# Merged products for shared edge tiles, split last units and a node-major output in a four-layer sparse graph network

## The chip, the cores and the metric

The kernel runs on one core of one Trainium2 chip. The metric is the device time of one execution in microseconds, and the figure for a kernel is the median of its runs. A profile is one further execution, taken with the hardware profiler.

## The reference

The input is `x`, 8 batches of 2048 nodes with 128 features each, and `adj`, one 2048 x 2048 matrix of 0 and 1. It is symmetric, has ones on its diagonal and about 16 ones in a row. Four layers follow one another; layers 0 and 2 are of one kind, 1 and 3 of another.

An attention layer (0 and 2) computes, in each batch,

```
Q, K, V = h Wq, h Wk, h Wv                       (8 heads of 16)
attn    = softmax over the neighbours m of n of Q[n].K[m] / 4
x       = LN1(h + (attn V) Wo + bo)
out     = LN2(x + relu(x W1 + b1) W2 + b2)
```

A graph layer (1 and 3) computes

```
h   = x W
e   = leaky_relu(h[i].a_src + h[j].a_dst)        for neighbours j of i
out = LN(x + softmax(e) h)
```

LN is a layer norm over the 128 features. All arithmetic is float32. The result is the output of layer 3, of shape (8, 2048, 128).

## The kernel before, in words

**Units and edge tiles.** The kernel doesn't use the dense adjacency. It first makes lists of neighbours from `adj`, and then works on 32 units of 64 nodes (`UNIT`, `NU`). On chip a unit's features are 128 rows: two halves of 64 rows, one for batches 0 to 3 and one for batches 4 to 7 (`HB` is 4, and `hf` counts the halves). Its columns are 4 batches x 128 features. A unit's nodes are two groups of 32 (`GROUP`, counted by `j`). Each group has edge tiles of 128 edges, and a unit has nine (`TILES`): four steps with one tile for each group, and a fifth step whose one tile is shared by both groups (`tiles = 1 if t == TG - 1 else 2`). An edge tile is gathered from a table in device memory, one row for one edge, by an indirect DMA that GpSimd issues (`gather`, L1469). The row of a node holds all 8 batches: keys and values for an attention layer (8 KB), or features with their two scores for a graph layer (4160 bytes).

**Attention layer.** For each step `spread` (L1542) multiplies one-hot matrices with the queries, so that each edge has its node's query in PSUM. VectorE multiplies it with the gathered keys (L1554) and sums over the head's 16 features (L1561). ScalarE takes the exponential (L1571). GpSimd or VectorE weighs the values with it (L1580). `add` (L1615) sums the edges of each node: a one-hot matrix of 128 edges x 32 nodes is multiplied with the weighted values and with the weights. For each group `j` and half `hf` this goes to its own strip of 32 rows of `acc` and `sums`.

**Graph layer.** VectorE and ScalarE make the weight of each edge and batch (L1788 to L1800), `fold` (L1810) multiplies the one-hot columns with them into `w`, and `add` (L1825) multiplies `w` with the gathered rows: for each batch, group and half one product of 128 edges x 32 nodes with 129 columns. For odd units the accumulators lie in the PSUM buffer `q` (four banks, one buffer), for even units in `acc` and `sums` (one bank each). Gathered rows of a graph layer go into a ring: one `kv` buffer holds four tiles, and there are six.

**After the sums.** `after_attention` (from L1626) divides, transposes, multiplies by Wo, adds the residual (`add_to`, L1649), normalises, runs the two-matrix network and normalises again. `after_graph` (from L1837) divides, adds the centred input (L1865) and normalises. In a norm, `centred` multiplies with a centring matrix on TensorE, `squares` takes each batch's variance (L1406 to L1409), `root` the inverse root (L1416, L1417), and four operations scale the four batches (L1439, L1441). Then `keep` (L1228) stores the unit's features in device memory (`xd`), `project` (L1328) multiplies with the next layer's weights, copies the rows out of PSUM into one of two `trows` buffers, and stores them in the next layer's table (L1392). In layer 3 the result, 64 nodes x 4 batches x 128 features for each half, is stored to the output instead (L1886), one 512-byte piece for each node and batch.

Most products of this part go to the PSUM tag `m`, which has two buffers of one bank. Operations after the sums run on ScalarE, except in the last two units of a layer (`late`), where `either` lets ScalarE or VectorE take them.

**What sets the order.** Operations are not issued where they are written. `op` records each with its estimated cost on each engine that can do it, a key (layer, then unit, then step), and the buffers it reads, writes or takes. `Plan.order` (L643) then runs a list scheduling: it keeps a clock, gives every free engine the ready operation of the lowest key for which the buffers are free, and so fixes each engine's order for the whole program. For the tags in `BY_KEY` buffers are given out in order of the keys. On the chip each engine follows this order. A gather of a layer reads the whole table of that layer, so that it waits until the last unit of the layer before has stored its rows.

Of the kernel before, what the change touches and what calls it, by code (L numbers as in the profile page):

```python
# [9 lines left out]
F32 = mybir.dt.float32  # L10
# [6 lines left out]
ALU = mybir.AluOpType  # L17
# [3 lines left out]
P = 128  # L21
H = 8
# [19 lines left out]
WIDE = DEG + 5  # L42
STRIDE = 1000
# [22 lines left out]
class Dense:  # L66
# [460 lines left out]
    def batch(self, b):  # L527
        x = self.two.tile([P, self.NB, P], F32, name="x")
        self.nc.sync.dma_start(out=x, in_=self.x_in[b].rearrange("(t p) d -> p t d", p=P))
        for n, kind in enumerate(LAYERS):  # L530
            if kind is MHA:
                units = 2 * self.NB * (self.N // QC)
                gen = self.attention(x, n)
            else:
                units = self.NB * self.NC
                gen = self.graph(x, n)
            for u in gen:
                yield u / units
        self.nc.sync.dma_start(out=self.out[b].rearrange("(t p) d -> p t d", p=P), in_=x)
# [14 lines left out]
class Cell:  # L554


    def __init__(self, tag=None, make=None):
        self.tag, self.make = tag, make
        self.tile = None
        self.writers, self.readers = [], []  # L560
        self.left = 0
        self.owner = None

# [11 lines left out]
class Plan:  # L575
# [12 lines left out]
    def __init__(self, nc):  # L588
        self.engines = {
            "PE": nc.tensor,  # L590
            "DVE": nc.vector,
            "ACT": nc.scalar,
            "POOL": nc.gpsimd,
            "SP": nc.sync,
        }
        self.ops = []
        self.bufs = {}
        self.pools = {}
        self.lines = set()
# [11 lines left out]
    def op(self, costs, fn, key, reads=(), writes=(), joins=(), holds=(), shares=(), port=False, dma=0):  # L611


        o = Op(costs, fn, key, port, dma)
# [127 lines left out]
class Sparse:  # L742
# [15 lines left out]
    def __init__(self, ctx, tc, x, xt, adj, w, out):  # L758
# [22 lines left out]
        self.late = False  # L781
        self.gates = {}
# [407 lines left out]
    def slots(self, e, hot, owner):  # L1190
# [3 lines left out]
            hot.tile[:, GS:HOT].rearrange("p (j t c) -> p t j c", j=2, t=TG),  # L1194
# [30 lines left out]
    def keep(self, u, x, key):  # L1225
        self.op(
            {"SP": 0.45},
            lambda e: e.dma_start(out=self.xd[u], in_=x.tile),  # L1228
            key,
            reads=[x],  # L1230
            writes=[self.x_at[u]],
            dma=P * CH * 4,
        )
# [51 lines left out]

    def copy(self, e, out, in_):
        if e is self.nc.scalar:
            e.copy(out, in_)  # L1288
        else:
            e.tensor_copy(out, in_)  # L1290

    def transposed(self, x, key, out, tag="m"):

        ps = self.cell(tag, [P, CH], name="ps_t")

        def run(e):
            for b in range(self.HB):
# [5 lines left out]
    def centred(self, x, key, *out):  # L1303

        ps = self.cell("m", [P, CH], name="ps_c")

        def run(e):
            for b in range(self.HB):
# [6 lines left out]
    def product(self, w, x, key, name, out):  # L1315

        ps = self.cell("m", [P, CH], name=name)
# [10 lines left out]
    def project(self, n, u, x, key, of=None, shares=()):  # L1328
# [5 lines left out]
        rows = self.cell(("trows", "hidden", "trows")[u % 3] if n == 0 else "trows", [P, hb * width], name="trows")  # L1334
        for v in range(2):
            tag = ("m", "m", "acc", "m", "m", "sums")[(2 * u + v) % 6] if n == 0 else "m"
            ps = self.cell(tag, [P, 2, 256], name="ps_p")

            def products(e, ps=ps, v=v):
                for b in range(2):  # L1340
                    cols = slice((2 * v + b) * P, (2 * v + b + 1) * P)
# [11 lines left out]
            if mha:  # L1353
# [9 lines left out]
                    writes=[rows],  # L1363
                )
            else:

                def fill(e, ps=ps, v=v):
# [10 lines left out]
                    writes=[rows],  # L1378
# [7 lines left out]
                    writes=[self.t_at[u]],  # L1386
                )

# [9 lines left out]
    def norm(self, r, key):  # L1398

        hb = self.HB  # L1400
        var = self.cell("var", [P, hb, 2])
# [9 lines left out]
        for b in range(hb):  # L1411
            self.op(self.either(0.55, 0.4), lambda e, b=b: squares(e, b), key, reads=[r], joins=[var])
        rstd = self.cell("rstd", [P, hb])
# [6 lines left out]
        normed = self.cell("normed", [P, hb, P])  # L1420
        for b in range(hb):
# [21 lines left out]
    def scaled(self, rows, gamma, beta, tag, key):  # L1443
        x = self.cell(tag, [P, CH])
# [46 lines left out]
    def attention(self, n):  # L1491
# [3 lines left out]
        for u in range(self.NU):  # L1495
# [14 lines left out]
            for t in range(TG):  # L1510
# [39 lines left out]
                op({"PE": 1.2}, spread, key - 6, reads=[q, hot], writes=[qe])  # L1550
# [52 lines left out]
                def add(e, t=t, kv=kv, hot=hot, acc=acc, sums=sums, part=part, exps=exps, tiles=tiles):  # L1603
# [6 lines left out]
                    for out, rhs in ((acc.tile, part(kv, 1)), (sums.tile, weights)):  # L1610
                        for j in range(2):
                            for hf in range(2):
                                rows = slice((2 * hf + j) * GROUP, (2 * hf + j + 1) * GROUP)
                                col = GS + (j * TG + t) * GROUP
                                e.matmul(  # L1615
                                    out[rows, :],
                                    lhsT=hot.tile[:, col : col + GROUP],
                                    rhs=rhs[:, 2 * (j % tiles) + hf, :],
# [5 lines left out]
            self.after_attention(n, u, acc, sums, x, base)  # L1624

    def after_attention(self, n, u, acc, sums, x, base):  # L1626
        self.late = u >= self.NU - 2
        L, hb = self.layers[n], self.HB
        op, cell = self.op, self.cell
        key = base + TG  # L1630
        rc = cell("rc", [P, hb * H])

        op({"DVE": 0.35}, lambda e: e.reciprocal(rc.tile, sums.tile), base, reads=[sums], writes=[rc])
        a = cell("rows", [P, hb, P], name="a")

        def divide(e):
            e.tensor_tensor(
                a.tile.rearrange("p b (h d) -> p (b h) d", d=HD),
                acc.tile.rearrange("p (c d) -> p c d", d=HD),
                rc.tile.unsqueeze(2).to_broadcast([P, hb * H, HD]),  # L1640
# [5 lines left out]
        def add_to(r, ps, bias, other, key):  # L1646
            op(
                {"DVE": 0.72},
                lambda e: e.scalar_tensor_tensor(r.tile, ps.tile, bias, other.tile, ALU.add, ALU.add),  # L1649
# [5 lines left out]
        at = cell("at", [P, CH])  # L1655
        ps = self.transposed(a, key, at)
        op(self.either(0.6, 0.68), lambda e, ps=ps: self.copy(e, at.tile, ps.tile), key, reads=[ps], writes=[at])
        r = cell("r", [P, CH], name="r1")
        ps = self.product(L["Wo"], at, key, "ps_o", r)
        add_to(r, ps, L["bo"], x, key - 2)  # L1660
        normed = self.norm(self.centred(r, key), key)
        x1 = self.scaled(normed, L["ln1_g"], L["ln1_b"], "x1", key)
        hidden = cell("hidden", [P, FFN // P, CH])
# [10 lines left out]
        r = cell("r", [P, CH], name="r2")  # L1674
        ps = cell("m", [P, CH], name="ps_y")
# [23 lines left out]
    def graph(self, n):  # L1699
# [3 lines left out]
        for u in range(self.NU):  # L1703
# [49 lines left out]
            if u % 2:  # L1753
# [13 lines left out]
            for i, t in enumerate(steps):  # L1767
# [36 lines left out]
                w = cell("w", [P, 2, 2 * hb, GROUP])  # L1804

                def fold(e, t=t, hot=hot, e8=e8, w=w, tiles=tiles):
                    oh = hot.tile[:, GS:HOT].rearrange("p (j t c) -> p j t c", j=2, t=TG)[:, :, t, :]
                    for j in range(0, 2, tiles):
                        shape = [P, tiles, 2 * hb, GROUP]
                        e.tensor_tensor(  # L1810
                            w.tile[:, j : j + tiles],
# [8 lines left out]
                def add(e, kv=kv, w=w, acc=acc, both_rows=both_rows, tiles=tiles, first=i == 0, last=i == TG - 1):  # L1820
                    for b in range(hb):
                        for j in range(2):
                            for hf in range(2):
                                rows = slice((2 * hf + j) * GROUP, (2 * hf + j + 1) * GROUP)
                                e.matmul(  # L1825
                                    acc(b)[rows, :],
                                    lhsT=w.tile[:, j, hf * hb + b, :],
                                    rhs=both_rows(kv)[:, j % tiles, hf * hb + b, 1 : P + 2],
# [6 lines left out]
            self.after_graph(n, u, outs, banks, acc, x, base)  # L1835

    def after_graph(self, n, u, outs, banks, acc, x, base):  # L1837
        self.late = u >= self.NU - 2
        L, hb = self.layers[n], self.HB
        op, cell = self.op, self.cell  # L1840
        key = base + TG

        rc = cell("rc", [P, hb], name="rcg")

        def inverse(e):
            for k, bank in enumerate(banks):
# [5 lines left out]
        a = cell("rows", [P, hb, P], name="a")  # L1852
        for b in range(hb):
            op(
                self.either(0.37, 0.28),
                lambda e, b=b: self.scale(e, a.tile[:, b, :], acc(b)[:, 0:P], rc.tile[:, b : b + 1]),
# [4 lines left out]
        r = cell("r", [P, CH])  # L1861
        ps = self.centred(x, key, r, a)
# [12 lines left out]
        else:  # L1875

            def last(e):
                shape = [P, 4, P]
# [5 lines left out]
            def store(e):  # L1884
                for part, nodes, hf in self.parts(u):
                    e.dma_start(  # L1886
                        out=self.out[hf * hb : (hf + 1) * hb, nodes, :].rearrange("b p d -> p b d"),
# [3 lines left out]
            op({"SP": 0.9}, store, key, reads=[normed], dma=P * CH * 4)  # L1891
# [101 lines left out]
```

## Time and profile before

| | us |
|---|---|
| median of 3 runs | 3263.28 |
| lowest and highest run | 3248.8, 3274.68 |
| the profiled execution's own time | 3296.99 |
| its span, first to last instruction | 3295.2 |
| layer 0, from the first gather (L1469) to the first of layer 1 | 136.2 to 1225.0 |
| layer 1, to the first gather of layer 2 | 1225.0 to 1789.7 |
| layer 2, to the first gather of layer 3 | 1789.7 to 2726.4 |
| layer 3, to the last output store's issue | 2726.4 to 3280.2 |

The page's mean granted TensorE clock is 0.867 of the full one. The DMA queue filled by the gathers moves 864 MB in 166,464 packets, the other data queue 155 MB in 94,464. TensorE's float32 products appear in the trace as two records each, and each has its own weight load ("PEld").

In the stage view each row is a stretch of time, with the busy microseconds and the number of instructions of each engine in it. In the timeline a row has a start, a duration, the engine, the line of the kernel, the operation, and what it writes and reads; "x8" merges eight records, and the square brackets say how long the engine had been idle before and what ended that. In the view of waits a row says which line waited for which, the total, how often, and the longest.

### The profile page before, as it was taken

What the parts mean: (1) busy time and instruction counts of PE and PEld (TensorE: products, weight loads), DVE (VectorE), ACT (ScalarE), POOL (GpSimd) and SP (SyncE); (2) the same over time, 40 slices, a digit from 0 to 9 for tenths busy, and PEclk for the clock granted to TensorE, in tenths of its full rate; (3) what the DMA queues carried; (4) which work ended last, traced back from release to release, by engine and by line L of the source; (5) the groups of instructions that cost most, each with busy time, mean ns of one, the idle gap of its engine ahead of it and who ended that gap; (6) DMA issues with size and microseconds to landing.
All of it is one profiled execution on the core that took longest, in us unless ns stands there. A gap on an engine that the chain in (4) does not pass through costs nothing. (4 is left out here: it accounts for less than half of the span.)

```text
span 3295.2 us, 63421 instructions
## 1 busy us (share of the span) xinstructions
PE 2532.1 (77%) x23624; PEld 1474.1 (45%) x23624; DVE 2311.1 (70%) x3617; ACT 1399.5 (42%) x4894; POOL 2104.5 (64%) x1447
## 2 busy tenths in 40 slices
PE   6777888878878866788876788888887785777675
PEld 5633444444334334565654233334443343555454
DVE  4789889878878763444444998998989873445554
ACT  4435455555444422444443244444444441333333
POOL 0168777777878835555563777878787835555552
PEclk8769889899999977888898899999999996778877
DMA  7868879887889749999997989999998848899994
GB/s 252 304 228 325 313 285 370 308 337 292 321 321 347 301 156 322 347 327 332 324 352 257 358 331 376 356 353 350 357 354 351 352 186 281 289 317 313 312 302 160
DMA packets 261246, 1023.15 MB, mean 310 GB/s; under 512 B 40193, under 2 KB 69633, under 8 KB 189025
## 3 DMA queue, kind: packets, MB, share of 16 engines
q0 software_dynamic: 166464, 864.44, 70.4%
q1 hardware_dynamic: 94464, 154.56, 13.7%
q8 instruction: 190, 3.11, 0.4%
q14 instruction: 128, 1.04, 0.1%
HBM read 978.59 MB, written 88.08 MB: 324 GB/s over the span
## 5 line engine op out<-in xcount | busy, mean ns | idle before, releaser
L1469 POOL DMA_INDIRECT kv<-table,idx x1152 | 1191.3, 1034 | 931.7 <-issue 395.9
L1580 POOL TENSOR_TENSOR kv<-kv 128x2048 f32<-128x2048 f32 (+1 forms) x252 | 900.0, 3584 | 76.8 <-ACT kv L1571 72.9
L1554 DVE TENSOR_TENSOR kv<-qe,kv 128x2048 f32<-128x2048 f32 (+1 forms) x320 | 662.7, 2071 | 184.6 <-DMA kv<-table,idx 117.2
L1561 DVE TENSOR_REDUCE s<-kv 128x128 f32<-128x2048 f32 (+1 forms) x320 | 659.4, 2061 | 11.4
L1542 PE MATMUL qe<-q_sb,hot 32*128 32x512 f32 (+1 forms) x2304 | 400.2, 700 | 193.7 <-DVE kv L1554 183.5
L1615 PE MATMUL acc<-kv,hot 128*32 128x512 f32 x2560 | 371.4, 658 | 55.1 <-POOL kv L1580 49.6
L1810 DVE TENSOR_TENSOR w<-hot,e 128x512 f32<-128x512 f32 (+1 forms) x384 | 222.2, 597 | 163.6 <-ACT e L1800 83.0
L1825 PE MATMUL acc_q<-kv,w 128*32 128x129 f32 x5120 | 264.7, 314 | 93.7 <-issue 66.7
L1825 PE MATMUL acc<-kv,w 128*32 128x129 f32 x2560 | 155.1, 330 | 135.2 <-issue 89.1
L1825 PEld LDWEIGHTS acc_q<-kv,w 128*32 128x32 f32 x5120 | 177.3, 124 | 166.7 <-issue 117.5
L1542 PEld LDWEIGHTS qe<-q_sb,hot 32*128 32x128 f32 (+1 forms) x2304 | 106.7, 197 | 319.3 <-DVE kv L1554 247.8
L1571 ACT ACTIVATE kv<-s 128x128 f32<-128x128 f32 (+1 forms) x320 | 95.1, 298 | 313.7 <-DVE s L1561 190.8
L1825 PE MATMUL sums<-kv,w 128*32 128x129 f32 x2560 | 171.6, 319 | 58.0 <-issue 57.3
L1406 ACT ACTIVATE junk<-ps_c 128x128 f32<-128x128 f32 x496 | 137.4, 277 | 175.6 <-PE ps_c L1310 116.0
L1288 ACT COPY trows<-ps_p 128x258 f32<-128x258 f32 (+1 forms) x230 | 108.3, 473 | 223.8 <-PE ps_p L1345 90.5
L1615 PEld LDWEIGHTS sums<-kv,hot 128*32 128x32 f32 x2560 | 88.8, 118 | 217.9 <-issue 214.6
L1320 PE MATMUL ps_f<-x,W 128*128 128x512 f32 x256 | 156.8, 700 | 20.5 <-ACT x L1449 12.1
L1825 PEld LDWEIGHTS acc<-kv,w 128*32 128x32 f32 x2560 | 86.4, 127 | 186.4 <-issue 120.0
L1800 ACT ACTIVATE e<-e 128x16 f32<-128x16 f32 (+1 forms) x320 | 65.6, 211 | 219.9 <-DVE e L1795 124.5
L1310 PE MATMUL ps_c<-centre,r 128*128 128x128 f32 x1024 | 145.7, 287 | 14.9 <-DVE r L1649 10.9
L1310 PEld LDWEIGHTS ps_c<-centre,r 128*128 128x128 f32 x1024 | 125.9, 194 | 67.1 <-DVE r L1649 32.3
L1679 PE MATMUL ps_y<-hidden,W 128*128 128x512 f32 x256 | 145.7, 654 | 3.3 <-DVE kv L1580 1.7
(170 smaller groups left out, 4052.4 us busy)
## 6 DMA issues: line engine op xcount, KB each, us to landing
table<-trows SPq DMA_DIRECT2D x128, 256.0 KB
xd<-xnew SPq DMA_DIRECT2D x96, 256.0 KB
x<-xd SPq DMA_DIRECT2D x96, 256.0 KB
kv<-table,idx POOLq DMA_INDIRECT x1152
table<-trows SPq DMA_DIRECT2D x128, 130.0 KB
kv<-adj_dram SPq DMA_DIRECT2D x16, 1024.0 KB
kv<-xt_dram SPq DMA_DIRECT2D x8, 1024.0 KB
x<-xt_dram SPq DMA_DIRECT2D x32, 256.0 KB
```

Source lines behind the costliest of these rows:

```text
L1310: e.matmul(ps.tile[:, cols], lhsT=flat(x.tile)[:, cols], rhs=self.centre, start=True, stop=True)
L1320: lambda e: e.matmul(ps.tile, lhsT=w, rhs=x.tile, start=True, stop=True),
L1406: e.activation(self.junk, x, AF.Square, scale=P**-0.5, accum_out=var.tile[:, b, 1:2])
L1469: e.indirect_dma_start(out=rows(kv.tile, j), out_offset=None, in_=self.tables[n], in_offset=bass.IndirectOffsetOnAxis(ap=self.idx[:, u, co ...
L1542: e.matmul(qe.tile[:, j, hf, :], lhsT=hot.tile[rows, t * P : (t + 1) * P], rhs=q.tile[rows, :], start=True, stop=True,)
L1554: e.tensor_tensor(k, qe.tile[:, 0:tiles].rearrange("p j h c -> p (j h) c"), k, ALU.mult)
L1561: e.tensor_reduce(s.tile[:, 0 : tiles * heads].rearrange("p (q c) -> p q c", q=2 * tiles), k, axis=mybir.AxisListType.X, op=ALU.add,)
L1580: e.tensor_tensor(v, v, w.unsqueeze(3).to_broadcast([P, 2 * tiles, heads // 2, HD]), ALU.mult)
L1615: e.matmul(out[rows, :], lhsT=hot.tile[:, col : col + GROUP], rhs=rhs[:, 2 * (j % tiles) + hf, :], start=(t == 0 and out is acc.tile), sto ...
L1679: lambda e, f=f, ps=ps: e.matmul(ps.tile, lhsT=L["W2"][:, f, :], rhs=hidden.tile[:, f, :], start=(f == 0), stop=(f == FFN // P - 1),),
L1810: e.tensor_tensor(w.tile[:, j : j + tiles], oh[:, j : j + tiles].unsqueeze(2).to_broadcast(shape), e8.tile[:, 0:tiles].unsqueeze(3).to_bro ...
L1825: e.matmul(acc(b)[rows, :], lhsT=w.tile[:, j, hf * hb + b, :], rhs=both_rows(kv)[:, j % tiles, hf * hb + b, 1 : P + 2], start=first and b ...
```

## The change

The change has three parts.

1. **One product for a shared tile.** Both groups' one-hot columns of a step now stand beside one another (in `hot`, and in `w` for the graph layers). Where a step's tile is shared, `add` makes one product with 64 output rows for each half, in place of two with 32 rows.
2. **The last unit's operations in two halves of the batches.** `in_halves` calls `after_attention` or `after_graph` twice for unit 31 of each layer: for batches 0 and 1 of each half, then for batches 2 and 3. Every operation has then half the columns; costs for the scheduling are multiplied by 0.55. Both use the same buffers on chip, each its part of the columns (`rows`, `Part`). The first half's products go to `m` as before, the second half's to `q` (`bank`). Rows go to the table when both halves are there. To leave `q` free for this, even units of a graph layer now accumulate in `q`, and odd ones (31 is odd) in `acc` and `sums`; and the scheduling lets `spread` of an attention layer start only when the layer's table is complete.
3. **Output by node.** The output lies in device memory as (node, batch, feature), so that a store of four batches writes 2048 bytes in one piece for each node (1024 in the halves of the last unit). The host returns a transposed view.

```diff
@@ class Plan / op
-        o = Op(costs, fn, key, port, dma)
+        o = Op({e: us * self.share for e, us in costs.items()}, fn, key, port, dma)
+        shares = [*shares, *(c.whole for c in (*reads, *writes, *joins, *holds) if c.whole)]
@@ slots
-            hot.tile[:, GS:HOT].rearrange("p (j t c) -> p t j c", j=2, t=TG),
+            hot.tile[:, GS:HOT].rearrange("p (t j c) -> p t j c", j=2, t=TG),
@@ new
+    def in_half(self, v, made):
+        self.blocks, self.made, self.at, self.plan.share = range(2 * v, 2 * v + 2), made, 0, 0.55
...
+    def bank(self, name, shape=None):
+        shape = shape or [P, len(self.blocks) * P]
+        if self.made is None or not self.blocks.start:
+            return self.cell("m", shape, name=name)
...
+        return Part(self.cell("q", [P, QB, CH], name=name + "_q"), cut)
@@ project
+        if halves[-1] == 0:
+            return
         def store(e):
@@ attention: spread
-                op({"PE": 1.2}, spread, key - 6, reads=[q, hot], writes=[qe])
+                op({"PE": 1.2}, spread, key - 6, reads=[q, hot, self.table[n]], writes=[qe])
@@ attention: add
-                        for j in range(2):
+                        for j in range(tiles):
                             for hf in range(2):
-                                rows = slice((2 * hf + j) * GROUP, (2 * hf + j + 1) * GROUP)
-                                col = GS + (j * TG + t) * GROUP
+                                at = (2 * hf + j) * GROUP
+                                rows = slice(at, at + GROUP * (3 - tiles))
+                                col = GS + (2 * t + j) * GROUP
                                 e.matmul(
                                     out[rows, :],
-                                    lhsT=hot.tile[:, col : col + GROUP],
-                                    rhs=rhs[:, 2 * (j % tiles) + hf, :],
+                                    lhsT=hot.tile[:, col : col + GROUP * (3 - tiles)],
+                                    rhs=rhs[:, 2 * j + hf, :],
...
-            self.after_attention(n, u, acc, sums, x, base)
+            self.in_halves(u, lambda: self.after_attention(n, u, acc, sums, x, base))
+
+    def in_halves(self, u, after):
+        self.late = u >= self.NU - 2
+        if u < self.NU - 1:
+            after()
+            return
+        made = []
+        for v in range(2):
+            self.in_half(v, made)
+            after()
+        self.whole()
@@ graph
-            if u % 2:
+            if u % 2 == 0:
                 outs = [cell("q", [P, 4, CH], name="acc_q")]
...
-                w = cell("w", [P, 2, 2 * hb, GROUP])
+                w = cell("w", [P, 2 * hb, 2, GROUP])
@@ graph: add
-                        for j in range(2):
+                        for j in range(tiles):
...
-                                    acc(b)[rows, :],
-                                    lhsT=w.tile[:, j, hf * hb + b, :],
-                                    rhs=both_rows(kv)[:, j % tiles, hf * hb + b, 1 : P + 2],
+                                    acc(b)[at : at + GROUP * (3 - tiles), :],
+                                    lhsT=w.tile[:, hf * hb + b, j : j + 3 - tiles, :].rearrange("p j c -> p (j c)"),
+                                    rhs=both_rows(kv)[:, j, hf * hb + b, 1 : P + 2],
@@ after_graph: store
+                    batches = slice(hf * hb + blocks.start, hf * hb + blocks.stop)
                     e.dma_start(
-                        out=self.out[hf * hb : (hf + 1) * hb, nodes, :].rearrange("b p d -> p b d"),
+                        out=self.out[nodes, batches, :],
                         in_=normed.tile[part],
                     )
```

## The prediction

> **What bounds the kernel now.** I read the page first (busy shares and the chain that ended last), then busy time by stage, then the timeline at the layer boundaries, then the waits inside the graph layers.
>
> ```profile
> PE 2532.1 (77%) x23624; PEld 1474.1 (45%) x23624; DVE 2311.1 (70%) x3617; ACT 1399.5 (42%) x4894; POOL 2104.5 (64%) x1447
> PE 13%; DVE 8%; issue 7%; DMA 6%; POOL 5%; another core or an unknown queue 2%; ACT 1%; POOLq 0%; SPq 0%; DVEq 0%; ACTq 0%
> ```
>
> No engine fills the span and the chain hops between all of them, so an average says nothing; the stages must be priced one by one. The stage view (columns: stretch, its length, then busy us and instructions of PE, PEld, DVE, ACT, POOL, then clock, DMA share, GB/s):
>
> ```profile
> 1190.10:1222.40 32.30, 24.05 (x78) 13.07 (x76) 16.36 (x39) 8.90 (x32) 0.00 (x0) 0.71 0.11 33
> 2692.70:2712.70 20.00, 16.49 (x71) 9.04 (x68) 12.69 (x33) 6.20 (x23) 0.00 (x0) 0.96 0.15 41
> 2712.70:2723.60 10.90, 4.70 (x20) 3.37 (x20) 4.15 (x11) 2.29 (x10) 0.00 (x0) 0.75 0.18 51
> 2723.60:2733.00 9.40, 0.00 (x0) 0.00 (x0) 0.00 (x0) 0.00 (x0) 5.08 (x6) 0.50 0.62 172
> 3272.70:3279.50 6.80, 2.02 (x12) 1.76 (x8) 4.63 (x16) 2.73 (x10) 0.00 (x0) 0.75 0.00 1
> 1300.00:1700.00 400.00, 321.39 (x4543) 234.32 (x4541) 177.08 (x657) 179.71 (x643) 224.88 (x218) 0.88 0.95 337
> 2000.00:2600.00 600.00, 500.31 (x3692) 236.53 (x3694) 534.56 (x337) 282.99 (x1003) 475.24 (x272) 0.95 0.92 357
> 2800.00:3200.00 400.00, 287.95 (x4289) 213.99 (x4288) 205.38 (x696) 143.94 (x576) 229.98 (x218) 0.78 0.91 308
> ```
>
> Attention (2000 to 2600) is bound by DVE, busy 89%. The graph layers (1300 to 1700, 2800 to 3200) have DVE near half, DMA at 0.95 and 0.91, PE at 80% and 72%. The first five rows are the ends of layers: POOL is silent, DMA nearly so, because the next layer's gathers need the whole table. The end of layer 2 in the timeline:
>
> ```profile
> 2712.70 0.75 DVE L1649 SCALAR_TENSOR_TENSOR r<-ps_y,b,x 128x512 f32<-128x512 f32 x1 [0.35 <-PE ps_y L1679]
> ...
> 2722.44 1.09 SPq L1392 DMA_DIRECT2D table<-trows  x2
> 2726.40 1.02 POOL L1469 DMA_INDIRECT kv<-table,idx  x1 [48.42 <-issue]
> ...
> 2733.06 0.19 DVE L1788 TENSOR_TENSOR e<-te,kv 128x16 f32<-128x16 f32 x1 [10.64 <-DMA kv<-table,idx]
> ```
>
> Unit 31's last accumulation ends at 2692.7, its table rows are issued at 2722.44: a tail of 29.7 us, of which 2712.70 to 2722.44 (9.7 us) belongs to unit 31 alone. The 10.6 us to the first gathered data stay whatever happens.
>
> Inside the graph layers, 1300 to 1700:
>
> ```profile
> POOL kv L1469 <- PE acc_q L1825: 77.1, 28, 5.7
> PEld acc_q L1825 <- issue: 43.9, 80, 1.3
> ```
>
> The gathers wait for PE to release ring slots, and PE itself often stands for nothing that the profile names ("issue"). So PE is close to setting the pace there, together with DMA.
>
> **What the Trainium skill says.** TensorEngine Tiling, section Available Configurations: a 128x32 arrangement gives four independent tiles, 128x64 two; Key Properties: changing the mode drains the array. The trace has no 128x64 product; the nearest rows are those split by input rows:
>
> ```profile
> 2309.41 1.14 PE L1542 MATMUL qe<-q_sb,hot 32*128 32x512 f32 x8
> 2313.93 1.13 PE L1542 MATMUL qe<-q_sb,hot 64*128 64x512 f32 x4
> 3248.32 1.10 PE L1825 MATMUL acc_q<-kv,w 128*32 128x129 f32 x32
> ```
>
> Half the records, double the tile, the same time: agrees with "four or two at once". TensorE: Matmul & The Clock Gate, What's actually happening: an idle TensorE runs at half clock until some 3.4 us of work. Agrees: the clock of the dead stretch 2723.6 to 2733 is 0.50. DMA: Bandwidth & Descriptors, Specifications: full rate from 512 bytes up; the next part measures how far that holds here.
>
> **The change, part by part.** The profiled execution took 3296.99 us (span 3295.2 plus 1.8); the runs shown have a median of 3263.28, 34 us (1.0%) less. I form the difference in the profiled execution and take it off the median.
>
> *Halved tails.* Last stretch of layer 2, per half, with 256 columns for 512: add 0.75 to 0.42, centring product 1.16 to 0.58, variance (0.37 per block, engines taking turns) 1.45 to 0.7, root 0.57 unchanged, scaling 1.6 to 0.8, rest of the transposes 0.5 to 0.3, xnew 0.81 to 0.47, projection and copies 2.6 to 1.3: 9.4 becomes 5.1 for a half. The second half follows by one long step, about 1.2: 6.3, a gain of 3.1 to 3.3. (DVE's 256-column prices are estimates on the line through 0.35 for 128 and 0.81 for 512 columns.) The 20 us before it are shared with unit 30, which stays whole; DVE is busy 12.69 and PE 16.49 of 20, so I give it half of the same third: 3.3. Together 6.5 for layer 2, and the same for layer 0, whose tail runs from 1190.1 to 1221.3. Bounds: 2 (PE fills the shared stretch) to 10 each.
> Layer 1's tail, 1768.2 to 1784.9, ends on something else:
>
> ```profile
> 1782.96 0.58 ACT L1288 COPY trows<-ps_p 128x512 f32<-128x512 f32 x1 [2.17 <-DMA table<-trows]
> 1784.92 1.08 SPq L1392 DMA_DIRECT2D table<-trows  x2
> ```
>
> Unit 31's rows wait for a store of an earlier, unhalved unit to leave one of two buffers. I take 1.5 (0 to 5).
> Layer 3: from 3272.7 to 3279.5 DVE is busy 4.63 of 6.8; 1.0 (0 to 2). The 15 us after it are untouched.
> Sum: 6.5 + 6.5 + 1.5 + 1.0 = **15.5** (4 to 27).
> What halving adds: one more xd store on SP per layer (0.33 us each) and two more output stores (0.6 each). The first half's go out while the second computes; in the second half one xd store still stands before the table stores, as now. If they bunch, 0.3 to 0.6 us per layer. Layer 1's SP queue also carries five weight loads between 1776.46 and 1780.39; they stay where they are.
>
> *One product for a shared tile.* Per graph unit 16 of 160 accumulation matmul records and as many weight loads go; per attention unit 4 of 40 wide and 4 narrow ones. In attention the wide ones take 1.06 us for 8 in four tiles, and should take the same for 4 in two; DVE covers it anyway. In the graph layers 16 records at two at once, each half of the 0.145 that a 128-column product's record takes when alone (1.16 for 8), make 1.16 against 1.10 now: no array time gained. What can go is a tenth of PE's unnamed stalls at the accumulation: 66.7 + 89.1 + 57.3 = 213 us, a tenth 21; PE is one of several limits, so I take a third: **7**. Bounds: a tenth of busy and stall together (591 + 213), 80 us, which the DMA shares cap at about 77 (5% and 9% of some 550 each); the other way, no overlap at all, +83 (below).
>
> *Output by node.* In 2800 to 3200 against 1300 to 1700:
>
> ```profile
> q1 hardware_dynamic: 16538, 12.60, 10.0%
> ...
> q1 hardware_dynamic: 10386, 24.16, 16.6%
> ```
>
> 10.0% of 16 x 400 us is 640; 24 fetches of 128 packets of 2 KB at 0.09 to 0.10 (the second row's mean is 0.102 at 2.3 KB) are 280 to 310, so 48 stores x 256 packets of 512 bytes took 330 to 360: 27 to 30 ns (17 to 19 GB/s an engine, against 20 to 23 for the larger ones: the page's 512 bytes are nearly enough). Four cost about 115 ns against 95 for one of 2 KB: 4,096 x 20 ns / 16 engines = 5 us if DMA alone set layer 3's pace, none if it doesn't. I take **1.5**.
>
> *Edits at nothing.* The new order of one-hot columns and of w: the same elements per instruction. Graph accumulators swapped between odd and even units: the same instructions, and the wider q buffer is free for the second half's products. The query spread of an attention layer planned after the table: 1.1 to 2.1 us on PE, behind nothing but the gather, whose data in layer 2 land 13 us after the store; only if the gather took under 3 us would it show.
>
> Sum: 15.5 + 7 + 1.5 = 24. 3297 becomes 3273 in profile, **3239** against the median of 3263.3.
>
> **Rivals.** *PE paces the graph layers (22%).* For: gathers wait on PE, unnamed stalls of 56 and 91 us (its lines' "issue" added up) in those two stretches of 400, 14 and 23%. Against: DMA at 0.91 to 0.95. Then 9% fewer records give some 50 us there: 3263 - 17 - 50 = 3196.
> *Everything hidden (23%).* The tails wait for unit 30's whole operations and for buffers, the records were off the path: 5 us, 3258.
> *Slower: the wide tiles do not overlap (8%).* In each shared-tile step of a graph layer the 16 records run one after another, 16 x 0.145 = 2.3 us for 1.0, on PE, which has about 0.8 us per unit (5% of 16.7) unspoken for. 64 x 1.3 = 83, less 17 of the tails: 3329. It decides as soon as the step exceeds some 1.9 us; the 64-row record of 1.13 us speaks against it. *A worse list order (7%)* from changed costs and buffers: +35.
> *My forecast (40%)*: 3225 to 3252.
>
> Chances: faster by over 1% (about what a measurement here can tell from no change; under 3230.6) 0.22 and a third of 0.40: 0.35. Slower 0.15. Within: 0.50. Range 3195 to 3278: it leaves out half of the first rival and the slow ones, some 2 in 10 with the calmest of these inside.
>
> **What would show it.** Tails: layer 2's last accumulation to table store in 22 to 24 us for 29.7, layer 1's hardly shorter. The shared step: 128x64 records, 16 in about 1.1 us. Graph stretch per unit, 16.7 us, near 16.5; under 16 the PE rival holds, over 17.2 the slow one. Output packets of 2 KB, POOL's waits in layer 3 unchanged. The forecast is wrong if layers 1 or 3 change by over 20 us, or attention layers outside their tails at all.

## The result, and the profile after

The changed kernel takes 3232.83 us (median of 9 runs, 3221.64 to 3242.13) against 3263.49 for the kernel before in the same comparison (9 runs, 3248.64 to 3274.68): a ratio of 0.9909, 95% interval 0.9888 to 0.9929, or -30 us (-37 to -23). The forecast was 3239, with -24. The profiled execution took 3238.66 us, span 3236.9.

The page of the changed kernel, busy shares and the chain that ended last (PE is TensorE, DVE VectorE, ACT ScalarE, POOL GpSimd, SP SyncE, which issues the stores; "issue" is idle time in which an engine waits for nothing that the profile shows):

```profile
PE 2498.6 (77%) x22108; PEld 1466.4 (45%) x22108; DVE 2310.2 (71%) x3633; ACT 1407.1 (43%) x4915; POOL 2109.9 (65%) x1447
PE 15%; DVE 7%; issue 5%; DMA 5%; POOL 2%; ACT 2%; another core or an unknown queue 1%; SPq 0%; DVEq 0%; POOLq 0%; ACTq 0%
```

The shares have hardly moved; only the count of PE's records has (23624 to 22108): the merge takes 16 records from each of 64 graph units and 8 from each of 64 attention units. As before, the stages have to be read one by one. By stage (columns as in the forecast: length, then busy us and instructions of PE, PEld, DVE, ACT, POOL, then clock, DMA share, GB/s), the ends of layers 0 and 2, and then the two graph stretches:

```profile
1196.70:1222.70 26.00, 21.38 (x104) 13.71 (x103) 17.51 (x54) 11.13 (x41) 0.00 (x0) 0.91 0.15 42
2667.00:2691.50 24.50, 20.31 (x104) 13.01 (x102) 15.53 (x48) 10.27 (x41) 0.00 (x0) 0.96 0.18 50
...
1300.00:1700.00 400.00, 319.35 (x4402) 236.74 (x4399) 186.09 (x688) 189.79 (x678) 237.55 (x229) 0.91 0.96 354
2770.00:3170.00 400.00, 287.63 (x4148) 220.07 (x4145) 217.21 (x743) 153.31 (x615) 245.17 (x231) 0.79 0.93 327
```

POOL is still silent at the ends of layers 0 and 2. Layer 0's stretch takes 26.0 us, although it begins 2.6 us before the last accumulation ends; the one shown of before, which begins just after that point, took 32.3. PE has more records in it (104 for 78), but is busy for less (21.4 us for 24.1). In the graph layers POOL issued 218 gathers in 400 us before; now 229 and 231. Layer 2's tail in the timeline:

```profile
2667.16 1.91 PE L1683 MATMUL acc<-kv,hot 128*64 128x512 f32 x4
...
2692.95 1.09 SPq L1458 DMA_DIRECT2D table<-trows  x2
2696.66 1.02 POOL L1535 DMA_INDIRECT kv<-table,idx  x1 [42.20 <-DMA table<-trows]
```

The last accumulation ends at 2669.2, and the last two stores of table rows are issued from 2692.95 on. The table gives, from the traces, the tail of each layer, from the end of the last accumulation to the issue of the last store (in layer 3 to the last operation on `normed`), and its "body", between the first and the last accumulation, in us:

| layer | tail before | tail after | body before | body after |
|---|---|---|---|---|
| 0 | 32.0 | 23.9 | 1003.0 | 1014.3 |
| 1 | 17.3 | 16.4 | 535.0 | 508.9 |
| 2 | 30.2 | 24.3 | 884.9 | 885.7 |
| 3 | 6.7 | 5.2 | 538.3 | 511.9 |

The tails give 16.4 us. The bodies of the graph layers give 26 each in this pair of profiles, and that of layer 0 takes 11 back. But the pair is 58 us apart and the medians 31, because the profile of before is 33 us above its own median. So the tails explain about half of the measured gain; that the graph layers give the rest is what the experiments have to show. What waits for what there, after (columns: us in total, times, longest), in 1300 to 1660:

```profile
POOL kv L1535 <- PE sums L1906: 56.6, 27, 6.1
POOL kv L1535 <- issue: 47.7, 150, 2.0
POOL kv L1535 <- PE acc_q L1906: 32.9, 17, 3.9
```

and before:

```profile
POOL kv L1469 <- PE acc_q L1825: 72.5, 26, 5.7
POOL kv L1469 <- issue: 44.0, 138, 2.1
POOL kv L1469 <- PE sums L1825: 33.5, 17, 4.1
```

The gathers (L1469, now L1535) wait for the accumulation (L1825, now L1906) to free a ring slot: 106.0 of 360 us before, 89.5 after.

### The profile page after: what moved, and what is told of

Same layout as the page of the kernel before. It is cut to its first block, busy times and chain, and to the rows that moved or that the text cites. A ratio compares the mean times of both kernels' runs of the same rounds, so it can differ in the third digit from the quotient of the medians.

```text
span 3236.9 us, 60457 instructions
## 1 busy us (share of the span) xinstructions
PE 2498.6 (77%) x22108; PEld 1466.4 (45%) x22108; DVE 2310.2 (71%) x3633; ACT 1407.1 (43%) x4915; POOL 2109.9 (65%) x1447
## 3 DMA queue, kind: packets, MB, share of 16 engines
q14 instruction: 127, 1.04, 0.1%
## 5 line engine op out<-in xcount | busy, mean ns | idle before, releaser
L1535 POOL DMA_INDIRECT kv<-table,idx x1152 | 1195.0, 1037 | 862.7 <-issue 338.2
L1683 PE MATMUL acc<-kv,hot 128*32 128x512 f32 (+1 forms) x2304 | 366.1, 644 | 56.8 <-POOL kv L1646 50.2
L1906 PE MATMUL acc_q<-kv,w 128*32 128x129 f32 (+1 forms) x4608 | 266.2, 319 | 160.8 <-issue 117.0
L1906 PEld LDWEIGHTS acc_q<-kv,w 128*32 128x32 f32 (+1 forms) x4608 | 177.0, 129 | 238.6 <-issue 179.9
L1906 PE MATMUL acc<-kv,w 128*32 128x129 f32 (+1 forms) x2304 | 141.1, 313 | 63.0 <-DVE w L1890 36.3
L1683 PEld LDWEIGHTS sums<-kv,hot 128*32 128x32 f32 (+1 forms) x2304 | 89.6, 119 | 210.0 <-issue 207.6
L1906 PE MATMUL sums<-kv,w 128*32 128x129 f32 (+1 forms) x2304 | 154.0, 309 | 36.9 <-issue 36.6
L1378 PE MATMUL ps_f<-x,W 128*128 128x512 f32 (+1 forms) x256 | 150.3, 674 | 21.1 <-ACT x L1515 11.3
L1759 PE MATMUL ps_y<-hidden,W 128*128 128x512 f32 (+1 forms) x256 | 144.4, 649 | 2.7 <-DVE kv L1646 1.2
L1505 ACT ACTIVATE normed<-ps_c,rstd 128x128 f32<-128x128 f32 x492 | 143.2, 370 | 4.3 <-DVE normed L1507 2.6
```

The costliest lines, as they stand in the source:

```text
L1378: lambda e: e.matmul(ps.tile, lhsT=w, rhs=x.tile, start=True, stop=True),
L1535: e.indirect_dma_start(out=rows(kv.tile, j), out_offset=None, in_=self.tables[n], in_offset=bass.IndirectOffsetOnAxis(ap=self.idx[:, u, co ...
L1683: e.matmul(out[rows, :], lhsT=hot.tile[:, col : col + GROUP * (3 - tiles)], rhs=rhs[:, 2 * j + hf, :], start=(t == 0 and out is acc.tile), ...
L1759: lambda e, f=f, ps=ps: e.matmul(ps.tile, lhsT=L["W2"][:, f, :], rhs=hidden.tile[:, f, :], start=(f == 0), stop=(f == FFN // P - 1),),
L1906: e.matmul(acc(b)[at : at + GROUP * (3 - tiles), :], lhsT=w.tile[:, hf * hb + b, j : j + 3 - tiles, :].rearrange("p j c -> p (j c)"), rhs= ...
```

## The experiments

Four theories stand against one another. T1, the forecast: the tails 15.5, the merged product 7 spread over all layers, the output 1.5. T2: PE paces the graph layers, and the merged product is worth 15 to 50 us there alone. T3: the exchange of the accumulators, or another order of the lists, gives the graph layers' gain. T4: the packets of 512 bytes held the gathers of layer 3 up.

### The parts one at a time: first chip

Merged products alone on the kernel before (the attention layers' `add` likewise, and the layout of the one-hot that both need):

```diff
-w = cell("w", [P, 2, 2 * hb, GROUP])
+w = cell("w", [P, 2 * hb, 2, GROUP])
...
-    for j in range(2):
+    for j in range(tiles):
         for hf in range(2):
...
-            acc(b)[rows, :],
-            lhsT=w.tile[:, j, hf * hb + b, :],
+            acc(b)[at : at + GROUP * (3 - tiles), :],
+            lhsT=w.tile[:, hf * hb + b, j : j + 3 - tiles, :].rearrange("p j c -> p (j c)"),
```

> The kernel before with the merged product alone (and the one-hot and weight layouts that it needs); its lists of instructions stand in the order of before. Forecast of the prediction: -7 us, a part of it in every layer, tails as before (32, 17, 30 and 7 us from the last accumulation to the last of the unit's work). PE-paces theory: -15 to -50 us, all of it between the first and the last accumulation of layers 1 and 3, where a unit goes from 16.6 to about 15.8 us, and nothing in layers 0 and 2. Order theory (the graph layers gain from the exchanged accumulators or another order of the lists): within 5 us of before.

Halves, with the exchange and the spread behind the table, but neither merge nor output:

```diff
-self.after_graph(n, u, outs, banks, acc, x, base)
+self.in_halves(u, lambda: self.after_graph(n, u, outs, banks, acc, x, base))
...
-if u % 2:
+if u % 2 == 0:
     outs = [cell("q", [P, 4, CH], name="acc_q")]
```

> The kernel before with the last unit's operations in two halves (the accumulators of even and odd units exchanged and the spread behind the table, as the halves need), without the merged product and with the output as before. Forecast: -16 us, all in the tails (layer 0 32 to 24, layer 2 30 to 24, layers 1 and 3 by 1 to 2 us each); the stretch between first and last accumulation of layers 1 and 3 as before. Order theory: about -30 us, with layers 1 and 3 some 10 to 25 us shorter between first and last accumulation.

Output by node alone:

```diff
-out=self.out[hf * hb : (hf + 1) * hb, nodes, :].rearrange("b p d -> p b d"),
+out=self.out[nodes, hf * hb : (hf + 1) * hb, :],
```

> The kernel before with the output by node alone; every engine but SP has the list of before. Forecast: -1.5 us, all of it in layer 3, 0 in layers 0 to 2. Output theory (packets of 512 bytes held the gathers of layer 3 up): -5 to -25 us in layer 3. Layers 0 to 2 are those of the kernel before, so they also say whether the trace of before is typical: layer 1 between first and last accumulation again 535 us if it is, about 520 if it was a slow sample.

The exchange alone:

```diff
-if u % 2:
+if u % 2 == 0:
```

> The kernel before with the two sets of accumulator banks exchanged between even and odd units of the graph layers, and nothing else. Forecast: 0, within 5 us. Order theory: -15 to -50 us, in layers 1 and 3 alone, a unit at about 15.8 instead of 16.6 us.

Measured, against 3061.43 us of the kernel before on this chip: merged 1.0018 (1.0002 to 1.0035), +5 us; halves 0.9957 (0.9940 to 0.9973), -13; output 0.9994 (0.9979 to 1.0008), -2; exchange 1.0003 (0.9989 to 1.0016), +1 (-3 to +5).

The first surprise is the time of the kernel before: 3061, where it had taken 3263. The 200 us lie almost wholly in the graph layers: layer 1's body is 442.1 us here (the run with the output changed, whose layers 0 to 2 are those of before) and was 535.0; layer 0's is 1007.4 and was 1003.0. A unit takes 13.8 us instead of 16.7 (in layer 3 12.8 instead of 16.8). The waits and the busy times of 1300 to 1660 in that run:

```profile
POOL kv L1469 <- DMA kv<-table,idx: 50.5, 74, 2.7
POOL kv L1469 <- issue: 34.5, 111, 0.8
POOL kv L1469 <- DVE w L1810: 9.7, 11, 2.0
...
1300.00:1660.00 360.00, 290.56 (x4956) 233.61 (x4949) 191.37 (x690) 194.95 (x691) 236.71 (x230) 0.88 1.02 402
```

On this chip the gathers wait 50.5 us for earlier gathers, and 2.0 us for the accumulation; DMA runs at 1.02 and 402 GB/s, against 0.95 and 335 in the profile of before. PE's accumulation shows hardly any unnamed idle time. Where the gathers hardly wait for PE, T2 expects no gain, so that it was neither shown nor refuted; it asks for a chip like that of the first comparison. T3 and T4 found nothing here. The halves gave -13 (-18 to -8), with tails of 24.2, 16.4, 24.3 and 5.2 us beside 28.7, 17.3, 29.5 and 6.8 us in the output run.

### Whole, undone and split: a chip like that of the first comparison

> The changed kernel whole, again. If the graph layers run at some 13.8 us per unit, as in the first four runs here: parts add up, theory 'the merged product helps only where PE paces': -10 us (-12 of the halves, -2 of the output, +3 of the merge), against -31 in the first comparison, with the bodies of layers 1 and 3 as before (440 and 409 us). If they run at 16.6 us as in the trace of before: -31 again, with 10 to 26 us less in each of the two bodies. Rival (the parts together free something that no part frees alone): -20 us or more even at 13.8 us per unit.

The change without the merge (the first diff above undone; halves, exchange and output stay):

> The changed kernel with the products of a shared tile split again (and the layouts as before); halves, exchange and output stay. Theory: at 13.8 us per unit within 5 us of the changed kernel, on the faster side of it, -14 us to before; at 16.6 us per unit 10 to 25 us slower than the changed kernel, all of it in layers 1 and 3. The forecast's own step said 7 us slower than the changed kernel.

The merge in the graph layers alone: the attention layers keep four products, with the new layout of the one-hot.

```diff
-col = GS + (j * TG + t) * GROUP
+col = GS + (2 * t + j) * GROUP
```

> The kernel before with the merged product in the graph layers alone (both layouts as in the change; the attention layers keep their separate products). Theory: 0 within 3 us at 13.8 us per unit, -10 to -30 at 16.6 us per unit. Against the next run: if the loss of the merged kernel (+2.5 us) is a cost of wide records in the attention layers, it isn't here.

The merge in the attention layers alone: `w` and the graph products as before, which read the new layout of the one-hot.

```diff
-lhsT=hot.tile[:, col : col + GROUP],
-rhs=rhs[:, 2 * (j % tiles) + hf, :],
+lhsT=hot.tile[:, col : col + GROUP * (3 - tiles)],
+rhs=rhs[:, 2 * j + hf, :],
```

> The kernel before with the merged product in the attention layers alone (layout of the one-hot as in the change; graph products and their weights as before). Theory: +3 to +6 us, in the bodies of layers 0 and 2: there two records of 64 columns took 654 ns (41.9 us over 128 records, by pairs) where four of 32 took 600 ns (147.3 us over 1024), 0.05 us a tile, 64 tiles a layer. The forecast said a gain of some 3 us here, a third of PE's unnamed stalls.

This chip, the experiments' second, takes 3270.47 us for the kernel before. Measured: the whole change 0.9905 (0.9873 to 0.9937), -31 us; without the merge 0.9956 (0.9939 to 0.9974), -14; the merge in the graph layers alone 0.9900 (0.9873 to 0.9927), **-33**; in the attention layers alone 1.0015 (1.0001 to 1.0029), **+5**. So the gain of the graph layers is the merge, T2: it comes with the merge alone, without exchange or output, and goes when the merge goes, although exchange and output stay. That leaves T3 and T4 nothing on this kind of chip either. The graph layers of the last run, unmerged, have bodies of 531.1 and 530.1 us; the whole change without the merge 527.0 and 523.0; merged alone 518.0 and 506.9; the whole change 513.7 and 511.6. The parts add up to -42 where the whole gave -31 (-42 to -21): whether something overlaps is not settled. One rival was not run alone: the new layout of `w` comes with the merge. Nothing in the traces speaks for it: in 1300 to 1660 the fold into `w` takes 690 ns in the run with the graph layers merged and 688 in the profile of before, and a weight load of 32 columns 113 to 120 and 119 to 121 ns.

### Instructions or array time?

The merge takes instructions away; does it also take array time, the time in which the products and their weight loads occupy TensorE? Merged, the shared tile in the timeline of the run with the graph layers merged, and the lines of the merged kernel on the first experiment's chip, where PE isn't waited for (busy us, mean ns):

```profile
1395.32 1.11 PE L1825 MATMUL acc_q<-kv,w 128*64 128x129 f32 x16
```

```profile
L1826 PE MATMUL acc_q<-kv,w 128*32 128x129 f32 x1664 | 60.1, 291 | 13.8 <-DVE w L1811 13.4
...
L1826 PE MATMUL acc_q<-kv,w 128*64 128x129 f32 x208 | 16.2, 305 | 0.0
...
L1826 PEld LDWEIGHTS acc_q<-kv,w 128*32 128x32 f32 x1664 | 46.1, 115 | 25.1 <-DVE w L1811 19.7 <-issue 1.7 <-DVE r L1866 1.3
...
L1826 PEld LDWEIGHTS acc_q<-kv,w 128*64 128x64 f32 x208 | 13.5, 155 | 2.6 <-DVE hot L1193 1.0 <-issue 0.8 <-DVE e L1796 0.3
```

16 wide records take 16 x 16.2 / 208 = 1.25 us, the 32 narrow ones that they replace 32 x 60.1 / 1664 = 1.16. The weight loads take 16 x 13.5 / 208 = 1.04 us for 32 x 46.1 / 1664 = 0.89. So no array time is gained. What goes is 16 of 160 records of products in a unit, and as many of weight loads. The opposite experiment has less array time with the same instructions; it leaves out the first 64 features in four of a unit's five steps:

```diff
-acc(b)[rows, :],
+acc(b)[rows, 0 if first else P // 2 :],
...
-rhs=both_rows(kv)[:, j % tiles, hf * hb + b, 1 : P + 2],
+rhs=both_rows(kv)[:, j % tiles, hf * hb + b, 1 if first else 1 + P // 2 : P + 2],
```

> The kernel before with as many products in the graph layers, but in four of the five tiles of a unit each moves 65 columns instead of 129 (the first 64 features of those tiles are left out of the sums). What is saved is array time alone: 32 products took some 1.1 us, so 160 take 5.5 us a unit, and four fifths of them at half the columns save up to 2.2 us. Theory 'the number of PE's instructions sets the pace' (at 16.6 us per unit): within 0.5 us a unit of before, -15 to 0 us in all. Rival 'array time sets it': 14.4 to 15.5 us a unit, -35 to -70 us in all. At 13.8 us per unit (gathers set the pace) both say nothing changes.

and half of the gathers' bytes. The products and the scores read the half row twice, and the indices are not doubled, so that the half rows also come from the first half of the table:

```diff
-out=rows(kv.tile, j),
+out=rows(kv.tile, j)[:, some],
...
-in_=self.tables[n],
+in_=self.tables[n].rearrange("n (h d) -> (n h) d", h=2) if n in (1, 3) else self.tables[n],
```

> The kernel before with every gather of layers 1 and 3 fetching 2080 instead of 4160 bytes a row (the second half of the batches computes on the data of the first, every engine's instructions stay). Theory 'PE's pauses of 0.5 to 0.8 us come with the traffic of the gathers': at 16.6 us per unit the pauses go and a unit falls to 13 us or less, -100 us or more in all. Rival 'PE pauses by itself': a unit stays at 15.5 to 16.6 us and the pauses stay, -35 to 0 us. At 13.8 us per unit: below 13 us, since there the gathers set the pace.

These two fell on a third chip, which is like the first experiment's: 3054.57 us before. Narrow products 0.9991 (0.9973 to 1.0009): nothing, as both theories had it there. Half a gather 0.9814 (0.9760 to 0.9867, four runs), -57 us, a unit at 12.3 us in layer 1 (from 13.8) and 12.5 in layer 3 (from 12.8): on this kind of chip the gathers set the pace of layer 1, by their bytes or by the stretch of the table that they read, and the next limit is close behind. Whether PE's pauses would go with fewer bytes on the other kind of chip was not tried.

The narrow products again, and the best of the parts, the change with the attention layers unmerged:

```diff
-for j in range(tiles):
+for j in range(2):
     for hf in range(2):
...
-lhsT=hot.tile[:, col : col + GROUP * (3 - tiles)],
+lhsT=hot.tile[:, col : col + GROUP],
```

> The kernel with 65 instead of 129 columns in four of five tiles of the graph layers' products again (it leaves out the first 64 features of those tiles), now hoped for on a chip that takes 16.6 us per unit. Theory 'the number of PE's instructions sets the pace': -15 to 0 us, pauses of 0.5 to 0.8 us as many as before. Rival 'array time sets it': -35 to -70 us. At 13.8 us per unit as in its first run: 0 within 5 us.

> The changed kernel with the products of the attention layers split again (the graph layers keep the merged product; halves, output and layouts stay). Theory: 3 to 6 us faster than the changed kernel on any chip, since the merge in the attention layers cost 5 us by itself: -34 to -38 us to before at 16.6 us per unit, -13 to -18 us at 13.8. Rival (the +5 us of the attention layers was the noise of one comparison): as the changed kernel, -31 or -10.

This was a fourth chip, with 3296.46 us before and a unit at 16.7. Narrow products: 0.9983 (0.9969 to 0.9997), -6 us (-10 to -1), bodies 534.4 and 535.7. The stage and waits of 1300 to 1660:

```profile
1300.00:1660.00 360.00, 276.52 (x4054) 209.29 (x4056) 157.23 (x585) 159.69 (x570) 203.70 (x195) 0.72 0.95 336
POOL kv L1469 <- PE acc_q L1825: 65.9, 24, 5.4
POOL kv L1469 <- PE sums L1825: 40.1, 20, 3.7
```

Against the profile of before, which is from the first comparison's chip (291.05 us of PE, 195 gathers, clock 0.87, 106 us of waits for the accumulation): the same gathers, the same waits. The accumulation's own busy time in layer 1's body fell from 258.7 to 207.8 us. Part of that is lost again at the lower clock (the products of the step left whole took 383 ns in the mean, and 307 before), and PE as a whole is busy 14.5 us less in the stretch, or 5%. If PE's busy time set the pace, 14.5 of every 360 us would be some 43 us over both bodies (an estimate); measured are 6. So array time doesn't set this pace. Fewer instructions with the same array time do save. Where they save can be seen in PE's own timeline, before:

```profile
1402.21 0.74 PE L1825 MATMUL acc_q<-kv,w 128*32 128x129 f32 x17
1403.24 0.42 PE L1825 MATMUL acc_q<-kv,w 128*32 128x129 f32 x4 [0.29 <-issue]
1403.99 0.30 PE L1825 MATMUL acc_q<-kv,w 128*32 128x129 f32 x2 [0.33 <-issue]
1404.72 0.51 PE L1825 MATMUL acc_q<-kv,w 128*32 128x129 f32 x9 [0.42 <-issue]
```

and in the narrow run, where the array has even less to do:

```profile
1384.40 0.27 PE L1825 MATMUL acc<-kv,w 128*32 128x65 f32 x2 [0.43 <-issue]
1385.12 0.22 PE L1825 MATMUL acc<-kv,w 128*32 128x65 f32 x1 [0.44 <-issue]
1385.85 0.27 PE L1825 MATMUL sums<-kv,w 128*32 128x65 f32 x1 [0.40 <-issue]
1386.55 0.66 PE L1825 MATMUL sums<-kv,w 128*32 128x65 f32 x12 [0.44 <-issue]
```

A group of products that depend on nothing more comes in handfuls, one every 0.7 us. Call it a stop when 0.45 to 0.8 us pass between the starts of neighbouring PE instructions (products or weight loads), and count the stops in the bodies of layers 1 and 3:

| traces | stops | us in them |
|---|---|---|
| slower kind of chip, graph layers not merged (before, without the merge, merged in attention alone, narrow) | 390, 383, 382, 387 | 243, 231, 230, 247 |
| slower kind of chip, graph layers merged (after, whole again, merged in graph alone, attention unmerged) | 348, 306, 343, 337 | 211, 186, 208, 213 |
| quicker kind (the four parts and the narrow products) | 38 to 47 | 23 to 31 |

With the merge the stops go down by about an eighth and the time in them by 33 us in the mean, about what the bodies lose (33 us in the mean of the same traces) and what the merge in the graph layers alone measured. (The limits are a choice: with 0.4 to 1.0 us it is 44 us.) The narrow products leave the stops as they were. A place that has to wait for the next instruction rather than for the array is a reading that fits both experiments; what keeps the instructions back on two of the four chips is not shown.

The change with the attention layers unmerged: 0.9880 (0.9849 to 0.9912), -40 us (-50 to -29, five runs). It is ahead of the kernel before by more than the whole change was in either comparison (-30 and -31), but the intervals overlap and the two did not run on one chip. The traces point the same way: the bodies of layers 0 and 2 are 1011 and 883 us in the mean of the four with merged attention layers, 999 and 878 in the mean of the ten without, though single ones overlap. The 5 us are likely, not shown.

## Why the prediction was right, and where it wasn't

**Tails, 15.5.** Right in sum and by layer: 8.1, 0.9, 5.9 and 1.5 in the profiles for 6.5, 1.5, 6.5 and 1.0; timed alone -13 (-18 to -8), with the output -14 (-20 to -9) on the other kind of chip. Reckoned as the forecast did, to the first of the last two stores, layer 2's tail is 23.8 us, within the 22 to 24 named. Layer 1's was hardly shorter, and the wait for an earlier unit's store is still in it (1.11 us, from 2.17). Part of layer 0's 8.1 is chance: the unhalved kernels' tails there were 28.1 to 32.0.

**Merged product, 7.** The step about array time was right: 16 wide records in 1.11 us, as long as 32 narrow ones; at 0.07 us a record they go two at once, against the 0.145 of one alone, as the Trainium skill's TensorEngine Tiling (Available Configurations) says of 128x64. What failed is the size: of a tenth of PE's unnamed stalls, 21 us, the forecast took a third, because "PE is one of several limits". In the graph layers it was -33 (-42 to -24) alone, more than the full tenth; taken out of the whole change it cost 17 (the ratios 0.9905 and 0.9956). There was no reason to take a third: on this kind of chip the gathers waited 106 of 360 us for the accumulation, and with the merge the time in stops fell by about as much as the bodies. The line that the forecast showed, 77.1 us of gathers waiting for `acc_q`, weighed more than the DMA share of 0.95: that share stood at 335 GB/s, and on the other kind of chip, where the gathers hardly wait for PE, the transfers run at 402. And the attention layers, of which the forecast said "DVE covers it anyway", lost 5: two intervals just above zero, and a size that fits the records there (layer 0 of the changed kernel, 1024 narrow in 147.3 us and 128 wide in 41.9: eight at 0.144 against four at 0.327 are 1.15 and 1.31 us a unit, at most 0.16 x 64 = 10). Whether the drain between tiling modes that the forecast cites has a part in it, no run here shows.

**Output, 1.5.** -2 (-6 to +2): the size can't be told from nothing. In both profiles of the first pair layer 3 changed as layer 1 did, which has no output, and that agrees.

**Edits at nothing.** The exchange: +1 (-3 to +5), right where it was run. The halves contain the later spread, and its price is not visible in their -13. The layouts weren't tried alone; with the new one-hot and old products the graph bodies are 531 and 530.

**Rivals and signs.** The rival "PE paces the graph layers" had the mechanism on the slower kind of chip, and its size was too large: it gave 9% fewer records some 50 us, where 17 to 33 came. By the forecast's own sign, a unit under 16 us, it stood on the edge: 15.9 and 16.0 in layers 1 and 3 of the first profile, 16.1 and 16.0 of the second. "Everything hidden" and the two slow ones fell; the order rival's stand-in, the exchange, did nothing. The forecast called itself wrong if layers 1 or 3 changed by over 20 us, or attention layers outside their tails at all. The first pair of profiles says 26 and 28 for the graph layers, the second comparison 17.5 and 20.3 (543.7 and 540.2 for the whole change, 561.2 and 560.5 for unmerged graph layers), and the attention layers probably lost 5. So its account of where the merge works did not hold. The time held because the tails were right and the merge's miss was small: in the whole change some 17 for 7, with 14 instead of 17 from tails and output. In part that was also luck with the chip: on the quicker kind the parts measured -13, +5 and -2, so that the whole would have gained about 10 us there (an estimate; it was not run).

## What to carry to other kernels

When two engines and the DMA all look nearly full, ask whom the next transfer waits for: here that wait, not the busy share, named the pace, and it differed between chips for one and the same program. Reduce instructions and array time separately to see which of the two a busy TensorE is short of. Where it was the instructions, merging two products into one of twice the width paid even though the array gained nothing; where it was neither, the wider product cost a little. Halving the last unit's chain at a layer's end gave about what its operations' durations said, on both kinds of chip (-13, and -14 with the output).

## What the runs showed of the hardware that was not expected

- The same program took 3061 and 3055 us on two chips, 3270 and 3296 on two others, steadily within a comparison. Each chip was seen in one comparison, so that chip and occasion can't be told apart. Nearly all of the difference is in the graph layers (an unmerged unit at 12.8 to 13.8 us or 16.3 to 16.8), while the bodies of the attention layers agree to some 1%. On the slower kind, the 4160-byte packets of the gathers are more often long (in layer 1, 6.4% over 0.25 us in the profile of before, against 1.3% in the output run), and PE's instructions come in handfuls 0.7 us apart. The two don't coincide in time: in layer 1 of before, 6.5% of the packets begun during a stop are long, and 6.4% of the others. What they have in common stays open.
- With half the columns in most products of the graph layers the granted clock in 1300 to 1660 was 0.72 on the slower kind of chip (0.87 in the profile of before) and 0.80 on the quicker kind (0.88 in the output run), at hardly a change in time.
